# Writing TensorE's order in the first stage of a decoder layer by hand

## The chip, the cores and the metric

The kernel runs on one core of a Trainium2 chip. The time is device microseconds of one execution. A core has several engines that run side by side, each with its own queue of instructions, executed in order: TensorE (PE in the profile) multiplies matrices, VectorE (DVE) does elementwise work and reductions, ScalarE (ACT) applies functions and copies, GpSimd (POOL) does some elementwise work here, and SyncE (SP) issues most of the transfers between memory and the on-chip buffers. An instruction that needs another engine's result waits at the head of its queue, and everything behind it waits too.

## The reference

One decoder layer with three sub-layers, each followed by a residual add and a layer normalisation. `x` has the shape (8, 512, 512) and the context (8, 512, 1024).

```
q, k, v = split(x @ W_in.T + b_in)              # 16 heads of 32
p  = pos @ W_pos.T + b_pos                      # relative positions
ac = einsum('tbhd,sbhd->bhts', q + r_w_bias, k) # t, s: 8 rows of the first axis
bd = rel_shift(einsum('tbhd,rhd->bhtr', q + r_r_bias, p))
attn = softmax((ac + bd) / sqrt(32))
x1 = layernorm(x + einsum('bhts,sbhd->tbhd', attn, v) @ W_out.T + b_out)

k, v = split((ctx @ W_src.T + b_src) * mask)    # 8 heads of 64, 512 keys
q    = (x1 @ W_tgt.T + b_tgt) * mask
u    = softmax(q k / 8, masked keys left out) v
x2   = layernorm(x1 + concat(x1, u) @ W_xout.T + b_xout)

out  = layernorm(x2 + ffn(x2))                  # 512 -> 2048 -> 512, quantised to fp8 between
```

The first attention goes over the first axis, which has only 8 entries: for each of the 512 rows of the second axis, 16 heads, 8 queries and 8 keys. The second attention goes over 512 keys, with a context of 1024 features.

## The kernel before, in words

The kernel has two stages. The first does the first attention, with its output projection, residual and normalisation, and beside it the keys and values of seven of the eight contexts. The second does the rest. Only the first stage is touched.

**The attention of the first stage** goes in NJ = 4 blocks `j` of 128 rows, each with T = 8 tiles `t` of 128 x 512. For a block, TensorE computes eight key products (`ps_k`, function `project`, L212), eight query products (`ps_q`) and eight value products (`ps_v`), each of four float32 matmuls of 128x512, and for each tile a small product `bd` (L378) with the relative positions. ScalarE copies keys and values to on-chip memory. VectorE does all of the attention by elementwise work, since 8 x 8 scores for each row are too small for TensorE: for each tile it adds a bias to the query (`qw`, L374), then for each half of the heads multiplies it with all keys (`pq`, L388) and sums over 32 features (`sc`, L397); every four tiles it adds `bd` (L405). GpSimd adds a constant `gc` (L416). Then comes the softmax of the block: maximum and subtraction on VectorE (L419 on), Exp on ScalarE (L423), sum, reciprocal and division on VectorE (L425 on). Then for each tile and half the scores are multiplied with all values (`pv`, L437) and summed in three adds (L447, L450, L453), which gives `ao`.

**The output** of a tile follows: TensorE transposes `ao` in four parts (`aot`, L458), ScalarE copies the result (`aoT`, L460), TensorE multiplies it with the output weights (`po`, L463). SyncE loads the row of `x` (L472), GpSimd adds the bias `bo` to it (L473), VectorE adds `po` (L479) and takes the statistics (L98, L99). Every four tiles ScalarE and VectorE make the inverse deviations (L103, L105), VectorE normalises (L109) and ScalarE's queue stores the result to `x1d` in memory.

**The set-up** projects the positions (`pp`, L283), combines them with the query weights (`pg` L320, `pc` L330 and L332) into `gp` and `gc`, and folds the value bias through the output weights into `bo` (`pbo`, added at L357). Columns that are needed as matrices are replicated by VectorE into two tiles, `brep` and `brew` (L328, L331, L347), which are used again and again.

**The context products of the first stage.** Contexts 0 to 5 are taken in three pairs. Keys (part 0) and values (part 1) of a pair are computed in two halves with seven products each instead of eight (a Winograd scheme, L553: `py`, `pz`, `px`): 2 x 3 x 2 x 7 = 84 products, each of the size of a key product (8 records in the profile, as each float32 matmul of this form is told as two). The scheme needs sums of weights (`sums_of_a`, L134 on) and of contexts (`sums_of_b`, L140 on), made by VectorE; those of the contexts are written to memory (`td`) and read again for part 1. ScalarE moves the results out of the accumulators (`put`), VectorE adds them (`add`, L595), and ScalarE's queue stores them to `kd` and `vd`. Context 6 is done in plain form by `project_context` in eight pieces of two products' length (`psk` L158, `psv` L172); its weights take the place of the keys and values of the last block (`w6k`, `w6v`), and its context the place of the tiles of `x`. Context 7 is done in the second stage.

**What sets the order.** In the first stage the program is written tile by tile, and the context products behind all blocks; a scheduler of the programming framework then puts every engine's instructions in an order that it plans by its own estimate of their durations, with a few pieces marked `high_priority`. In the second stage the orders of TensorE, VectorE, ScalarE and SyncE are those in which the program issues the instructions (`manual_schedule`).

**Buffers.** Accumulators in the first stage: two for the products of `x` (`ps_mm`), one each for `bd`, `aot` and `po`, three for set-up and context products (`ps_kv`). `qw`, `ao` and `aoT` have two buffers each, `pq`/`pv` one, `r` four, and the tiles of `x` eight. Keys, values and scores have one buffer each, so that a block's keys can be written only when the scores of the block before are done, and its values when the last `pv` is done.

At the end of the stage, SyncE's queue waits for the last `pv` of block 3 before it loads the value weights of context 6, then come `w_src`, the second stage's weights and, by way of memory, the transposed `x1` (`x1Ts`), with which the first product of the second stage (`psq`, L824) begins.

Of the kernel before, what the change touches and what calls it, by code (L numbers as in the profile page):

```python
# [17 lines left out]
P = 128  # L18
# [24 lines left out]
def decoder_layer(  # L43
# [22 lines left out]
    nc = tc.nc  # L66

# [11 lines left out]
    def col(i):  # L79
        return colv[:, i : i + 1]  # L80
# [49 lines left out]

    A11, A12, A22, S3, S1, S2, S4 = range(7)
# [17 lines left out]
    def project_context(t, w_k, w_v, ct_of, ps_pool, ps_tag, st_pool, st_tag):  # L149
# [5 lines left out]
        def keys(o):  # L155
            ps = ps_pool.tile([P, S], F32, tag=ps_tag, name=f"psk{t}_{o}")
            for f in range(FC):
                nc.tensor.matmul(  # L158
                    ps,
                    lhsT=w_k[:, f, o * P : (o + 1) * P],  # L160
# [8 lines left out]
        def values(s):  # L169
            ps = ps_pool.tile([P, E], F32, tag=ps_tag, name=f"psv{t}_{s}")  # L170
            for f in range(FC):
# [3 lines left out]
                    rhs=w_v[:, f, :],  # L175
# [11 lines left out]
    with ExitStack() as ph:  # L187
# [33 lines left out]
        def keys_of(j):  # L221

            k_all = kvp.tile([P, T, E], F32, tag="k", name=f"k{j}")
            xts = []
            for t in range(T):
                xt = xtp.tile([P, EC, P], F32, tag="xt", name=f"xt{j}_{t}")

                (nc.sync if j else nc.scalar).dma_start(xt, xT[t, j])
                xts.append(xt)
                ps = project(xt, 1, f"k{j}_{t}")  # L230
                nc.scalar.copy(k_all[:, t, :], ps)
            return xts, k_all
# [7 lines left out]
        first = keys_of(0)  # L240
# [10 lines left out]
        with tc.tile_pool(name="setup", bufs=1) as sp:  # L251
# [26 lines left out]
            for z in (pz, pzb, zb):  # L278
                nc.gpsimd.memset(z, 0.0)
            for c in range(EC):  # L280
                pp = ps_kv.tile([P, 15], F32, tag="kv", name=f"pp{c}")
# [29 lines left out]

            one = sp.tile([P, P], F32, name="one")
            nc.gpsimd.memset(one, 1.0)
            brep = sp.tile([P, P], F32, name="brep")
            brew = sp.tile([P, P], F32, name="brew")

            for c in range(EC):
# [10 lines left out]
                nc.vector.tensor_scalar(brep, one, bqr[:, c : c + 1], None, ALU.mult)  # L328
                pg = ps_kv.tile([P, 4, 15], F32, tag="kv", name=f"pc{c}")
                nc.tensor.matmul(pg, lhsT=brep, rhs=pz[:, c], start=True, stop=False)  # L330
                nc.vector.tensor_scalar(brew, one, bwr[:, c : c + 1], None, ALU.mult)  # L331
                nc.tensor.matmul(pg, lhsT=brew, rhs=zb[:, c], start=False, stop=True)  # L332
                nc.scalar.copy(gc[:, 4 * c : 4 * c + 4, :], pg)

            for part in (0, 2):
                nc.sync.dma_start(
                    w_in[:, :, part * E : (part + 1) * E],
                    chunked(w_inT)[:, :, part * E : (part + 1) * E],
                )
            nc.scalar.dma_start(w_o, chunked(w_outT))  # L340

# [1005 lines left out]
```

## Time and profile before

| | |
|---|---|
| median of 3 runs | 2117.41 us (2115.08 to 2119.38) |
| the profiled execution, own time | 2119.34 us |
| its span, first to last instruction | 2117.6 us |
| first query add of VectorE | at 44.25 us |
| end of the last `ao` of the first stage | at 823.26 us |
| first product of the second stage | at 892.66 us |
| mean granted TensorE clock | 0.993 |
| PE, DVE, ACT, POOL busy in the span | 97%, 68%, 22%, 8% |

The busy time of PE counts a matmul from its start to its modelled end, and neighbouring matmuls overlap; back to back, a 128x512 record starts every 0.429 us while its own length is given as 0.6. A lone one therefore counts for more, and a busy share near 100% does not say that nothing more would fit. Windows give the busy time of every engine in a stretch of the span; the lists of waits give, for each engine, what it waited for at the head of its queue, with the total, the number of times and the longest. Waits of an engine that is not the bottleneck cost nothing. The costliest lines of VectorE in the first stage are L437 (64 of 2353 ns in the mean), L388 (64 of 2318 ns) and L397 (64 of 2280 ns).

### The profile page before, as it was taken

What the parts mean: (1) busy time and instruction counts of PE and PEld (TensorE: products, weight loads), DVE (VectorE), ACT (ScalarE), POOL (GpSimd) and SP (SyncE); (2) the same over time, 40 slices, a digit from 0 to 9 for tenths busy, and PEclk for the clock granted to TensorE, in tenths of its full rate; (3) what the DMA queues carried; (4) which work ended last, traced back from release to release, by engine and by line L of the source; (5) the groups of instructions that cost most, each with busy time, mean ns of one, the idle gap of its engine ahead of it and who ended that gap; (6) DMA issues with size and microseconds to landing.
All of it is one profiled execution on the core that took longest, in us unless ns stands there. A gap on an engine that the chain in (4) does not pass through costs nothing.

```text
span 2117.6 us, 17267 instructions
## 1 busy us (share of the span) xinstructions
PE 2058.4 (97%) x5768; PEld 881.4 (42%) x5768; DVE 1434.4 (68%) x2285; ACT 467.4 (22%) x955; POOL 173.3 (8%) x147
## 2 busy tenths in 40 slices
PE   9899999999999999998999999999999999999998
PEld 4444344444444444432434443434444434343443
DVE  3999999999999996057554754845747548356232
ACT  3011102110110111122223232332332323333211
POOL 0200010110012001010101111010010100000000
PEclk9999999999999999999999999999999999999999
DMA  6421341345015254576493654745636537427200
GB/s 215 177 71 40 142 151 30 120 188 194 25 55 203 94 187 156 183 194 159 109 224 91 118 131 96 138 111 95 135 88 110 139 91 143 104 65 156 53 20 20
DMA packets 246201, 255.27 MB, mean 121 GB/s; under 512 B 141024, under 2 KB 161504, under 8 KB 246112
## 3 DMA queue, kind: packets, MB, share of 16 engines
q1 hardware_dynamic: 228736, 223.45, 41.4%
q10 hardware_dynamic: 17376, 30.71, 4.1%
q8 instruction: 46, 0.75, 0.1%
q14 instruction: 43, 0.35, 0.1%
HBM read 130.36 MB, written 56.62 MB: 88 GB/s over the span
## 4 chain that ended last, share of the span: by engine, by line
PE 69%; DVE 22%; DMA 5%; issue 2%; SPq 1%; ACT 1%; POOL 0%; ACTq 0%; DVEq 0%; POOLq 0%
PE h L1036 21%; PE pox L981 5%; PE pox L969 5%; PE s L844 5%; PE av L944 5%; PE o L1053 4%; PE px L553 4%; PE psq L824 4%; DVE pq L388 4%; DVE sc L397 4%; DVE pv L437 4%; DVE pv L447 2%; PE psk L158 2%; PE psv L172 2%; PE ps_q L212 2%
## 5 line engine op out<-in xcount | busy, mean ns | idle before, releaser
L1036 PE MATMUL h<-x2T,w 128*128 128x512 f32 x1024 | 454.4, 599 | 4.3 <-DVE x2T L752 4.3
L859 DVE CUSTOM_DVE_ANT_0 pe<-s,mb 128x512 f32<-128x512 f32 x256 | 162.0, 681 | 208.8 <-PE s L844 208.8
L1036 PEld LDWEIGHTS h<-x2T,w 128*128 128x128 f32 x1024 | 192.1, 191 | 263.1 <-issue 255.7
L869 ACT ACTIVATE pe<-pe,nmax 128x512 f32<-128x512 f32 x256 | 182.2, 712 | 202.4 <-DVE nmax L859 200.2
L896 DVE STREAM_TRANSPOSE pb<-pe 128x512 f32<-128x512 f32 x256 | 159.5, 678 | 0.0
L1043 ACT ACTIVATE hq<-h,colv 128x512 fp8e4<-128x512 f32 x128 | 87.9, 687 | 294.5 <-PE h L1036 294.5
L437 DVE TENSOR_TENSOR pv<-v,sc 128x2048 f32<-128x2048 f32 x64 | 150.6, 2353 | 2.0
L388 DVE TENSOR_TENSOR pq<-qw,k 128x2048 f32<-128x2048 f32 x64 | 148.4, 2318 | 1.2
L397 DVE TENSOR_REDUCE sc<-pq 128x64 f32<-128x2048 f32 x64 | 145.9, 2280 | 1.3
L844 PE MATMUL s<-kT,qTx 64*128 64x512 f32 x512 | 128.0, 616 | 3.6 <-DVE nmax L859 3.4
L212 PE MATMUL ps_q<-w_in,xt 128*128 128x512 f32 x256 | 121.4, 604 | 5.0 <-DVE qw L374 5.0
L944 PE MATMUL av<-pT,vx 128*64 128x512 f32 x512 | 119.1, 608 | 6.3 <-DMA raw<-vd 6.3
L212 PE MATMUL ps_k<-w_in,xt 128*128 128x512 f32 x256 | 116.7, 606 | 5.4 <-DMA xt<-in_xT_dram 4.9
L884 DVE TENSOR_SCALAR pe<-pe,rden 128x512 f32<-128x512 f32 x256 | 115.4, 493 | 4.5
L463 PE MATMUL po<-w_o,aoT 128*128 128x512 f32 x256 | 117.4, 601 | 0.7 <-ACT aoT L460 0.7
L824 PE MATMUL psq<-x1Ts,w_tgt 128*128 128x512 f32 x256 | 113.8, 597 | 1.7 <-DVE x1Ts L752 1.7
L981 PE MATMUL pox<-w_xo,uT 128*128 128x512 f32 x256 | 115.2, 598 | 0.0
L969 PE MATMUL pox<-w_xo,x1Ts 128*128 128x512 f32 x256 | 114.4, 596 | 0.0
L1053 PE MATMUL o<-w2q,hq 128*128 128x512 fp8e4 x512 | 114.1, 379 | 0.0
L212 PE MATMUL ps_v<-w_in,xt 128*128 128x512 f32 x256 | 112.0, 594 | 0.0
L473 POOL TENSOR_TENSOR r<-r,bo 128x512 f32<-128x512 f32 x32 | 57.5, 1822 | 507.8 <-DMA r<-in_x_dram 368.7
L988 DVE TENSOR_TENSOR x<-pox,x 128x512 f32<-128x512 f32 x32 | 22.1, 692 | 105.6 <-PE pox L981 67.7
(142 smaller groups left out, 2165.4 us busy)
## 6 DMA issues: line engine op xcount, KB each, us to landing
pT<-pb SPq DMA_DIRECT2D x512, 128.0 KB, 2.4
ch<-in_ctxT_dram SPq DMA_DIRECT2D x24, 512.0 KB, 6.7
td<-tx SPq DMA_DIRECT2D x12, 768.0 KB, 5.7
tx<-td SPq DMA_DIRECT2D x12, 768.0 KB, 8.2
r<-in_x_dram SPq DMA_DIRECT2D x32, 256.0 KB, 3.8
x1d<-r ACTq DMA_DIRECT2D x32, 256.0 KB, 2.6
x1Ts<-x1d SPq DMA_DIRECT2D x32, 256.0 KB, 5.7
kT<-kd SPq DMA_DIRECT2D x32, 256.0 KB, 3.2
```

Of the source, the lines that this page charges most:

```text
L212: nc.tensor.matmul(ps, lhsT=xt[:, e, :], rhs=w_in[:, e, part * E : (part + 1) * E], start=(e == 0), stop=(e == EC - 1),)
L388: nc.vector.tensor_tensor(pr, qw[:, fs] .rearrange("p (h d) -> p h d", d=D1) .unsqueeze(2) .to_broadcast([P, HH, T, D1]), k_all[:, :, fs]. ...
L397: nc.vector.tensor_reduce(sc[:, t, g * HH * T : (g + 1) * HH * T], pr.rearrange("p h s d -> p (h s) d"), AX.X, ALU.add,)
L437: nc.vector.tensor_tensor(pr, v_all[:, :, fs].rearrange("p s (h d) -> p s h d", d=D1), sc[:, t, g * HH * T : (g + 1) * HH * T] .rearrange( ...
L824: nc.tensor.matmul(ps, lhsT=w_tgt[:, e, o * P : (o + 1) * P], rhs=x1T[t][:, e, :], start=(e == 0), stop=(e == EC - 1),)
L844: nc.tensor.matmul(ps[:, h, :], lhsT=qT[t][half[h], c, j * P : (j + 1) * P], rhs=kT[t, c][half[h], :], start=True, stop=True,)
L869: nc.scalar.activation(pe, pe, AF.Exp, bias=nmax[:, h : h + 1], scale=-1.0, accum_out=den[:, h : h + 1],)
L944: nc.tensor.matmul(av[half[h], :], lhsT=v[t, c][:, s, half[h]], rhs=pT[t, c][:, :, :, s, h].rearrange("p g i q -> p (g i) q"), start=(s == 0),
L969: nc.tensor.matmul(po, lhsT=x1T[t][:, e, j * P : (j + 1) * P], rhs=w_xo[:, e, :], start=(e == 0), stop=False,)
L981: nc.tensor.matmul(po, lhsT=uT[t][:, e, j * P : (j + 1) * P], rhs=w_xo[:, EC + e, :], start=False, stop=(e == EC - 1),)
L1036: nc.tensor.matmul(ps, lhsT=w1[0][:, e, n * P : (n + 1) * P], rhs=x2T[t][:, e, :], start=(e == 0), stop=(e == EC - 1),)
L1053: nc.tensor.matmul(po, lhsT=hq[t][:, c, j * P : (j + 1) * P], rhs=w2q[:, c, :], start=(c == 0), stop=(c == HC - 1),)
```

## The change

TensorE's order in the first stage is now the order in which the program issues it; VectorE, ScalarE, GpSimd and SyncE are still ordered by the scheduler. The block's work is cut into functions of one tile: `keys`, `queries_of`, `offsets`, `values`, `softmax`, `weigh`, `turn_out` (transposes and copy) and `put_out` (projection, residual, normalisation). Their bodies are those of before.

The program keeps a planned time, `clock`. A slot has one of three lengths: SCORES for a query tile, SOFTMAX for the softmax of a block, VALUES for a tile of the weighted values. In a slot the listed steps are issued, with products of `spare` set between them (the values of this block, or the keys of the next), and the rest of its length is filled from `filling`, a generator that issues one context product at a time. The generator can also say that another product has to come between (`"between"`), or that no context product may be issued for a while (a negative number).

```
        SCORES, SOFTMAX, VALUES, FULL = 11.2, 13.0, 12.4, 3.54

        def slot(length, items, left):
            begin, due = due, due + length
            steps = list(items)
            for i in range(max(len(spare) - left, 0)):
                steps.insert(2 * i + 1, None)
            for i, step in enumerate(steps):
                if step:
                    must(*step)
                elif len(spare) > left:
                    must(FULL, *spare.pop(0))
                until = begin + length * (i + 1) / len(steps)
                if step and step[1] is turn_out:
                    until = max(until, clock + 0.5)
                fill(until)
            fill(due)
```

The blocks are then written so:

```diff
+        filling.append(context_work())
+        for j in range(NJ):
+            for t in range(T) if j else range(2, T):
+                if j and t == 0:
+                    spare += [(values, j, u) for u in range(T)]
+                items = []
+                if t < T - 1:
+                    items.append((FULL, queries_of, j, t + 1))
...
+                items += [(0.9, offsets, j, u) for u in late]
+                if j and t < 2:
+                    items.insert(0, (0.9, turn_out, j - 1, T - 2 + t))
+                    items.append((FULL, put_out, j - 1, T - 2 + t))
+                slot(SCORES, items, T - 1 - t)
+            softmax(j)
...
+                spare += [(keys, j + 1, u) for u in range(T)]
+            fill(clock + FULL)
+            slot(SOFTMAX, [], max(len(spare) - 2, 0))
+            for t in range(T):
+                weigh(j, t)
+                items = []
+                if t > 1:
+                    items.append((0.9, turn_out, j, t - 2))
+                if t == T - 1:
...
+                        items.append((FULL, queries_of, j + 1, 0))
+                if t > 1:
+                    items.append((FULL, put_out, j, t - 2))
+                slot(VALUES, items, max(T - 3 - t, 0))
```

So the query of a tile is issued one tile ahead; the transposes of a tile come two slots after its weighted values, those of the last two tiles of a block in the first two query slots of the next block; and the output projection of a tile stands at the end of the slot in which the tile was transposed, behind another product.

In block 3 there are no keys of a next block. The weights for the keys of context 6 are loaded after that block's softmax and for its values at its last tile, and the four key pieces of context 6 join the filling work behind the context products. After the last slot come the turn of tiles 6 and 7, each followed by filling work and its projection, then what is left, then the four value pieces.

The set-up is cut up too: all replicated columns are made at the start in tiles of their own, and TensorE's order is keys 0 to 5, `pp` 0, key 6, `pp` 1, key 7, `pp` 2 and 3, query 0; then, in the first two query slots, combination 0, query 1, combination 1, and combination 2, query 2, combination 3, the bias product `pbo`, with value products between them. Context products may be issued from 33.0 us of planned time after that.

```diff
+            reps = []
             for c in range(EC):
+                reps.append([])
+                for n, src in (
+                    ("r", bqr[:, c : c + 1]),
+                    ("w", bwr[:, c : c + 1]),
+                    ("v", colv[:, C_BV + c : C_BV + c + 1]),
+                ):
+                    rep = sp.tile([P, P], F32, name=f"rep_{n}{c}")
+                    nc.vector.tensor_scalar(rep, one, src, None, ALU.mult)
+                    reps[c].append(rep)
...
-                nc.vector.tensor_scalar(brep, one, bqr[:, c : c + 1], None, ALU.mult)
...
+            must(1.0, project_offsets, 0)
+            must(FULL, keys, 0, T - 2)
+            must(1.0, project_offsets, 1)
+            must(FULL, keys, 0, T - 1)
+            for c in (2, 3):
+                must(1.0, project_offsets, c)
+            must(FULL, queries_of, 0, 0)
```

The context products keep their order among themselves; the generator marks the places where it yields:

```diff
+                        y = bank("py")
+                        product(y, A12, b21, True)
+                        yield FULL
+                        if i == 0 and m + part > 0:
+
+                            yield -6.0 if part else -13.0
...
+                        add(0, 0, x)
+                        store(0, 0)
+                        yield "between"
+                        product(x, S2, t2, False)
+                        yield FULL
```

The number of instructions of each kind on each engine stays as it was.

## The prediction

> **What bounds the kernel now.** I read the busy shares first, then the slices, the windows by stage, the two wait lists of the first stage, and the timeline where it ends. Shares and slices (40 slices of 52.9 us):
>
> ```profile
> PE 2058.4 (97%) x5768; PEld 881.4 (42%) x5768; DVE 1434.4 (68%) x2285; ACT 467.4 (22%) x955; POOL 173.3 (8%) x147
> ...
> PE   9899999999999999998999999999999999999998
> ...
> DVE  3999999999999996057554754845747548356232
> ```
>
> PE looks full throughout, but VectorE is full in slices 2 to 16: that is the first stage, which alone is changed. Windows (length, PE busy, PEld, DVE, ACT, POOL, clock, DMA share, GB/s) from the first query add to the last attention output, and on to the second stage:
>
> ```profile
> 44.25:823.50 779.25, 750.55 (x2031) 342.90 (x2030) 746.36 (x669) 98.62 (x171) 78.89 (x64) 1.00 0.34 117
> 823.50:892.70 69.20, 69.20 (x164) 30.50 (x163) 7.73 (x14) 6.86 (x11) 3.87 (x2) 1.00 0.63 202
> ```
>
> DVE is idle for 32.9 of 779.25 us: up to `ao` the stage goes by VectorE. Then PE alone has 69.2 us left. What each waits for (us, times, longest), PE first:
>
> ```profile
> PE aot L458 <- DVE ao L453: 10.9, 10, 2.0
> PE ps_q L212 <- DVE qw L374: 5.0, 4, 1.5
> PE ps_k L212 <- DMA xt<-in_xT_dram: 4.9, 1, 4.9
> ```
>
> ```profile
> DVE den L425 <- ACT sc L423: 8.0, 4, 2.5
> DVE mx L419 <- POOL sc L416: 7.1, 4, 1.8
> DVE qw L374 <- PE ps_q L212: 5.9, 2, 3.9
> DVE r L479 <- POOL r L473: 2.5, 3, 1.4
> DVE st L595 <- PE px L553: 1.7, 2, 1.3
> DVE w L134 <- DMA w<-in_w_srcT_dram: 1.4, 1, 1.4
> ```
>
> 15.1 us are the softmax's own chain, some 13 us are waits on other work, the rest small gaps (4.8). The end of the stage on PE's timeline:
>
> ```profile
> 838.58 26.77 PE L158 MATMUL psk<-ct,w6k 128*128 128x512 f32 x62
> 865.19 27.63 PE L172 MATMUL psv<-w6v,ct 128*128 128x512 f32 x64
> 892.66 13.90 PE L824 MATMUL psq<-x1Ts,w_tgt 128*128 128x512 f32 x32
> ```
>
> From 838.58 to 865.19 are 62 matmuls, 0.429 us each: a product of 8 matmul records is 3.43 us, a piece of context 6 (16) is 6.87.
>
> **The change, part by part.** Nothing is added to the arithmetic; the order on PE, and through it the waits, are what changes. The second stage starts at 892.66 before; I work out where it starts after.
>
> *PE alone.* 229 products x 3.43 (786) + 32 offset groups x 0.89 (28.4) + 32 groups of transposes x 0.46 (14.7) + set-up 8.8 = 838 us. PE starts at 4.93 and the first products are 2.95 slower than warm ones, so it could not be done before 846: before, PE loses 46.6 us.
>
> *DVE alone.* It keeps its instructions: 746.4 busy, less some 2.0 (replicated columns, now made before the first query: 8 of 0.28, less their overlap) and 1.4 (one `r` add with its statistics, 0.68+0.68, put off until after `ao`) = 743.0. The first query is done after 8 key products, four `pp` of 0.88 and one product: 4.93+2.95+27.4+3.5+3.4, about 42.3; qw at 42.9 (before 44.25). Softmax waits 12.7: 15.1 less 2.4, as context adds can now stand in them (bounds 10 to 15). Small gaps 4.8. So the last `ao` lands at 42.9+743.0+12.7+4.8 = 803.4 plus X, where X is what DVE waits for PE and loads (13.1 before).
>
> *Where PE is last held by DVE.* I lay the after kernel's two instruction lists side by side with these durations. Without waits, PE comes to the turn of tile 2 in block 3 only 1.8 us after `ao` (tile 3: 2.2; tiles 5 to 7: 12 to 15). DVE's softmax waits and X come on top, so PE waits there, and behind it PE has more left than DVE. `ao` of tile 2 lies five value tiles ahead of the last; one is two halves of pv, add, add, add at 4.77 plus r and statistics, by the list 54 in all: 803.4-54 = 749.4+X. Behind that turn PE has 6 groups of transposes 2.8 + 6 output products 20.6 + 13 context products 44.6 + 8 pieces 55.0 = 123.0 us. End: 872.5+X.
>
> *X, by its waits.* Third qw, behind two combines and a product on PE: 0.9. `bo` waiting for pbo, now behind the fourth combine: 2.1. Sums waiting for w and the first context loads: 1.5 (the row shows 1.4; 0 to 3). The add of block 0's first pair waiting for pz, as PE does a product in between: 3.5 by the list (nearest row 1.3; 0 to 4). Third query of block 2, behind a turn, a projection and values: 2.0. `r` behind POOL: 1.5 (row: 2.5 in three). Sum 11.5. Not counted, as PE is then 5 to 17 us ahead in the list, and so the range's upper part: in block 0 PE holds at v3 until qw of tile 3, which stands behind the first pair's sums on DVE (4 to 7.5); at px behind a DVE add (2.5); at the fourth and fifth output projection, whose single bank waits for the r adds (2.7+1.1). Everything in PE's fixed queue then stands behind them: values, context products, queries.
>
> *The tensor clock.* A 4.35 us wait before the feed-forward product costs more than itself:
>
> ```profile
> 1923.70 13.18 PE L1036 MATMUL h<-x2T,w 128*128 128x512 f32 x24 [4.35 <-DVE x2T L752]
> ```
>
> 24 at 0.43 would take 10.5; so 2.7 more, and the windows say why (granted clock is the number after POOL):
>
> ```profile
> 1920.00:1925.00 5.00, 1.30 (x2) 0.79 (x3) 2.79 (x6) 0.16 (x1) 0.00 (x0) 0.72 1.29 202
> 1925.00:1930.00 5.00, 5.00 (x8) 1.94 (x8) 4.21 (x12) 2.10 (x3) 0.00 (x0) 0.60 1.04 237
> 1930.00:1935.00 5.00, 5.00 (x14) 2.13 (x12) 1.15 (x4) 3.48 (x8) 0.00 (x0) 1.00 0.88 278
> ```
>
> In the first stage no wait of PE passes 2.2 us once it runs. The new order has two long ones by the list, both in block 3: some 16+ us at tile 0's turn (absorbed, as PE is held again) and about 6 at tile 2's, after which PE is the bound. I take 2.2 there (between 0 and 2.7). [...]
>
> *What I cost at nothing.* POOL's 32 adds (57.5 us) and their interplay with DVE: pv takes 2353 ns in the mean, 2290 undisturbed; 64 of each make 4 us, so -4 to +4. SP's queue: key tiles, `r`, sums and context loads are issued in the new order, key products follow context products, so the x tiles (bound: one 4.9 us wait, the row for xt) come up to one product earlier than needed; 0 to 3. ACT's copies, 98.6 busy of 779: 0. The loads of context 6 go ahead of `ao`'s last tiles on SP, as they do before; its keys are wanted only some 20 us behind the loads: 0 to 3. At the stage's end SP waits for the last pv before the value weights, w_src and w_tgt; x1Ts is turned by DVE at 888.8, 3.8 us ahead of 892.66. The same order remains: after the last `ao` PE has po and 8 pieces, 58.9, where before it had 69.2. If the 10 us less cover is more than the loads bear: 0 to 5. I take 0, since the other half of that chain (last `ao`, stores, loads) also comes sooner.
>
> *Sum.* 872.5+11.5+2.2 = 886.2 against 892.66: -6.5 us. The profiled execution took 2119.34 (span 2117.6 and 1.74 around it), 1.9 above the median 2117.41; I put the difference on the median: 2110.9, say 2111.
>
> **Rivals.**
> A. *DVE walks freely.* The three slot lengths leave PE ahead everywhere, X is 0 to 5 and the clock keeps up. For it: before, PE's waits on ao and qw (15.9) are symptoms of an order which is now loosened by two slots; in blocks 1 and 2 the list gives PE 15 to 30 us of slack. Against: set-up and block 0. End 872.5 to 877.5: 2097 to 2102.
> B. *No difference.* One early stall of PE (v3, 7.5) is passed on through qw: 893.7, +1.0, 2118; or the transition's loads take 5: 2116.
> C. *Slower: a convoy in block 0.* PE's order cannot step past v3, px and the two output projections, DVE then waits for the queries behind them, and passes everything on, as it is the bound until block 3. Price 7.5+2.5+3.8 = 13.8 on top: end 900.0, +7.3, 2125. It is slower than before once X plus the clock passes 20.2, by over 0.2% past 24.4. For it: in block 0 the list has only 5 us to spare at tiles 4 and 5. Against: later blocks have 15 us and more, though slack of PE's side cannot win time back for DVE.
> D. *The order does nothing.* If DVE is the bound throughout and X stays at 13.1, only the tail changes: 872.5+13.1+2.2, -4.9, 2112.5; it falls in with the forecast.
>
> **How the numbers follow.** Forecast with D (2103 to 2113) 0.42; A 0.14; B (within 0.2%, 4.2 us, about what a measurement of this kernel can tell) 0.21; C 0.23. Faster: 0.42+0.14 = 0.56. The range leaves 0.1 at each end: down to A's 2098; up, C's 2125 with 2.7 for a second cold stretch and POOL's half: 2128. The forecast's own range is 2103 to 2116.
>
> **What would show it.** Right: psq of the second stage starts at about 886; last `ao` near 815; PE's list has lost aot but for block 3, with one wait of over 10 us there and a granted clock under 1 behind it near 760; DVE's waits on PE add to about 10. Wrong: waits of qw on ps_q repeated in every block (C); PE waiting in front of psk, or psq waiting on x1Ts or w_tgt (transition); a larger mean of pv or pq (POOL); second stage not 1225 us long.

## The result, and the profile after

The changed kernel is slower: a median of 2130.4 us (2124.54 to 2131.57, six runs) against 2118.37 us in the six runs beside it, a ratio of fast runs of 1.0047 with a 95% interval of 1.0032 to 1.0061 (the two medians alone give 1.0057). Forecast were 2111 us, and at most 2128. The profiled execution took 2124.54 us, the fastest of the six. A later one of the same kernel (run e8_again) took 2129.8, and is used beside it where the difference matters.

The page of the changed kernel, busy shares and slices (40 of 53.1 us; PEclk is the granted TensorE clock in tenths):

```profile
PE 2050.7 (97%) x5768; PEld 889.9 (42%) x5768; DVE 1439.9 (68%) x2285; ACT 467.1 (22%) x955; POOL 171.5 (8%) x147
...
PE   9999999999999879998999999999999999999998
...
DVE  4999999999899997157554754835747648356232
...
PEclk9999999999999989999999999999999999999999
```

The shares say nothing: 97% and 68%, as before. The slices do: PE has an 8 and a 7 in slices 14 and 15, where it had nines, and the clock an 8. That is 690 to 796 us, block 3's softmax and its first value tiles.

Windows from the first query add to the last `ao`, and on to the second stage (length, PE busy, PEld, DVE, ACT, POOL, clock, DMA share, GB/s):

```profile
41.46:831.97 790.51, 748.59 (x2027) 353.24 (x2026) 748.46 (x657) 98.38 (x171) 77.58 (x64) 0.98 0.33 116
831.97:901.05 69.08, 68.73 (x167) 30.64 (x165) 9.71 (x17) 6.87 (x11) 3.53 (x2) 1.00 0.64 204
```

VectorE starts 2.8 us earlier than before and its last `ao` lands 8.7 us later (831.97 against 823.26); what PE has left then is as long as before, 69.1 us against 69.4. What PE waits for in the first 900 us (us, times, longest):

```profile
PE aot L337 <- DVE ao L329: 19.4, 3, 11.9
PE po L346 <- ACT aoT L339: 8.2, 9, 2.5
PE ps_k L216 <- DMA xt<-in_xT_dram: 5.1, 1, 5.1
PE ps_v L216 <- DVE qw L245: 5.0, 1, 5.0
PE po L346 <- DVE r L362: 3.8, 3, 1.6
PE px L660 <- DVE st L702: 3.4, 3, 2.4
```

and VectorE between its first query add and its last `ao`:

```profile
DVE ao L329 <- PE aot L337: 7.1, 3, 4.2
DVE den L301 <- ACT sc L299: 6.8, 4, 2.5
DVE qw L245 <- PE ps_q L216: 6.7, 5, 3.9
DVE mx L295 <- POOL sc L292: 6.5, 4, 1.8
DVE r L362 <- PE po L346: 3.3, 4, 1.5
DVE bo L560 <- PE pbo L553: 1.9, 1, 1.9
```

Before, PE waited for `ao` twelve times in this stretch, 12.5 us in all and 2.0 at the longest. Now it waits three times, 11.9 the longest, and all three stand in block 3. The timeline of PE there:

```profile
725.83 3.60 PE L660 MATMUL pz<-ch,w 128*128 128x512 f32 x8
729.26 3.60 PE L660 MATMUL px<-cl,w 128*128 128x512 f32 x8
744.78 0.69 PE L337 MATMUL aot<-ident,ao 128*128 128x128 f32 x2 [11.93 <-DVE ao L329]
749.55 0.69 PE L337 MATMUL aot<-ident,ao 128*128 128x128 f32 x2 [4.08 <-DVE ao L329]
750.92 6.10 PE L346 MATMUL po<-w_o,aoT 128*128 128x512 f32 x8 [0.68 <-ACT aoT L339]
```

After `px` at 729.26 the order has nothing until the first turn of block 3, although context products are left: that `px` is followed by the mark for a product in between, and in block 3 no values or keys remain that could stand there. The planned time moves only when something is issued, so the pauses of the generator do not run out either. And the end of the stage:

```profile
852.98 20.76 PE L162 MATMUL psk<-ct,w 128*128 128x512 f32 x48
873.58 27.63 PE L176 MATMUL psv<-w,ct 128*128 128x512 f32 x64
901.05 13.90 PE L1002 MATMUL psq<-x1Ts,w_tgt 128*128 128x512 f32 x32
```

The second stage starts at 901.05 instead of 892.66, 8.4 us later. In the repeated execution it starts at 903.55, and the stage behind it is as long as before (1224.4 against 1224.9 us), so the 10 us lie in the first stage.

**A ledger of PE.** For every matmul of the first stage I take the time from its start to the next one's start, less the median for its form; the sum is what PE loses to waits and to a lower clock. The medians add up to 837.5 us in every kernel, as the matmuls are the same, and PE begins at 4.8 to 5.1. Together with the losses that gives the start of the second stage by construction, so the agreement is no proof; the ledger only says where the time is lost. In us:

| kernel | 0-100 | 100-700 | 700-800 | later | second stage at |
|---|---|---|---|---|---|
| before | 13.4 | 30.8 | 3.7 | 2.4 | 892.7 |
| changed, first profile | 9.4 | 18.0 | 28.2 | 2.8 | 901.0 |
| changed, repeated (e8_again) | 11.9 | 18.2 | 28.2 | 2.8 | 903.5 |
| PE's order planned (e9_planned) | 4.2 | 19.0 | 8.3 | 4.1 | 878.2 |
| by hand up to block 3's softmax (e12) | 9.6 | 17.8 | 8.3 | 3.7 | 881.8 |
| by hand from there on (e13) | 3.9 | 19.0 | 29.5 | 1.8 | 896.5 |
| before, with the new set-up (e14) | 3.3 | 35.3 | 2.4 | 3.8 | 887.2 |

The change does remove losses: 12.8 us of them between 100 and 700 us, and 1.5 to 4.0 in the first 100. It loses 24.5 us more than before in the one stretch behind.

### The profile page after: what moved, and what is told of

Its sections match the earlier page's. It is cut to its first block, busy times and chain, and to the rows that moved or that the text cites. A ratio compares the mean times of both kernels' runs of the same rounds, so it can differ in the third digit from the quotient of the medians.

```text
span 2122.8 us, 17257 instructions
## 1 busy us (share of the span) xinstructions
PE 2050.7 (97%) x5768; PEld 889.9 (42%) x5768; DVE 1439.9 (68%) x2285; ACT 467.1 (22%) x955; POOL 171.5 (8%) x147
## 4 chain that ended last, share of the span: by engine, by line
PE 77%; DVE 17%; DMA 2%; issue 2%; ACT 1%; SPq 1%; POOL 0%; ACTq 0%; DVEq 0%
PE h L1214 21%; PE pox L1159 5%; PE s L1022 5%; PE pox L1147 5%; PE av L1122 5%; PE px L660 5%; PE psq L1002 5%; PE o L1231 4%; PE po L346 3%; DVE pq L249 3%; PE ps_q L216 3%; PE ps_k L216 3%; DVE pv L313 3%; PE ps_v L216 3%; DVE sc L258 3%; PE psk L162 2%
## 5 line engine op out<-in xcount | busy, mean ns | idle before, releaser
L346 PE MATMUL po<-w_o,aoT 128*128 128x512 f32 x256 | 121.5, 619 | 11.9 <-ACT aoT L339 8.2
L216 PE MATMUL ps_v<-w_in,xt 128*128 128x512 f32 x256 | 117.5, 603 | 5.0 <-DVE qw L245 5.0
L216 PE MATMUL ps_q<-w_in,xt 128*128 128x512 f32 x256 | 115.3, 593 | 1.3 <-DVE qw L245 1.3
```

The source lines that it names most:

```text
L216: nc.tensor.matmul(ps, lhsT=xt[:, e, :], rhs=w_in[:, e, part * E : (part + 1) * E], start=(e == 0), stop=(e == EC - 1),)
L346: nc.tensor.matmul(po, lhsT=aoT[t][:, c * P : (c + 1) * P], rhs=w_o[:, c, :], start=(c == 0), stop=(c == EC - 1),)
```

## The experiments

VectorE's, ScalarE's, GpSimd's and SyncE's orders are planned anew for each kernel, so a small edit moves instructions on them too; that is a limit of all the small edits below. Times are medians of four to ten runs beside runs of the kernel before; the ratio is to that kernel.

**Three buffers for `ao`**

```diff
-            ao[t] = qp.tile([P, E], F32, tag="ao", name=f"ao{j}_{t}")
+            ao[t] = qp.tile([P, E], F32, tag="ao", bufs=3, name=f"ao{j}_{t}")
```

> ao has three buffers instead of two, nothing else is changed. Theory 1 (VectorE's waits for a free ao buffer, 7.1 us in three, are passed on to the end, as VectorE holds PE at the turn of tile 2 in block 3): the waits of ao on aot vanish, the last ao lands at 824 to 826 instead of 831.96, the second stage starts at 894 to 896 instead of 901.05, time 5 to 7 us below the changed kernel. Theory 2 (VectorE only waits elsewhere, since PE is behind at those places: on ps_q, po or r): the waits move to other lines, last ao within 2 us of 832, time within 2 us of the changed kernel.

2131.05 us, 1.0059 (1.0044 to 1.0074): no gain. The waits on `aot` are gone, and the first lines of VectorE's list of waits are now

```profile
DVE qw L245 <- PE ps_q L216: 15.0, 7, 4.1
DVE den L301 <- ACT sc L299: 6.8, 4, 2.5
DVE mx L295 <- POOL sc L292: 6.5, 4, 1.8
DVE r L362 <- POOL r L356: 4.2, 3, 1.9
```

`qw` has gone from 6.7 to 15.0. The last `ao` lands at 836.15, no earlier than in the repeated execution of the changed kernel (834.47). The buffer was only the place where VectorE met PE's delay; theory 2 holds.

**Nothing held back where nothing can stand in between**

```diff
-                if clock < rest or between or not filling:
+                if ((clock < rest or between) and spare) or not filling:
```

> The pauses of the context products hold only while there are other products to put in between; so block 3's softmax and its first value slots are filled with context products. Theory 1 (the end is set by PE's tail behind the turn of tile 2 in block 3, 128.7 us, with 19.4 us of idle PE ahead of it): PE's waits on ao fall from 19.4 to under 6 us, PE's work behind that turn to about 82 us, and the stage's end is then what follows the last ao: value pieces of context 6, psq between 870 and 890, time 11 to 30 us below the changed kernel, also below the kernel before by up to 18. Theory 2 (transfers at the end of the stage set it: value weights, w_src, x1Ts behind the last pv): the idle time moves behind the last ao, PE waits for w or x1Ts there, psq stays within 4 us of 901.

2123.56 us, 1.0024 (1.0014 to 1.0035): 6.8 us below the changed kernel, less than either theory's good case. PE's waits on `ao` are gone, but the products that moved up are those behind the boundary of two pairs of contexts, whose loads have only begun:

```profile
746.91 1.02 PE L660 MATMUL py<-ch,w 128*128 128x512 f32 x2
748.55 1.13 PE L660 MATMUL py<-ch,w 128*128 128x512 f32 x2 [0.62 <-DMA ch<-in_ctxT_dram]
756.19 2.08 PE L660 MATMUL py<-ch,w 128*128 128x512 f32 x2 [6.51 <-DMA ch<-in_ctxT_dram]
761.12 2.07 PE L660 MATMUL py<-ch,w 128*128 128x512 f32 x2 [2.85 <-DMA ch<-in_ctxT_dram]
```

The four parts of `ch` land one after another, and a product issued as a whole stands before each. PE still loses 18.0 us between 700 and 800, and the first turn comes at 793.73 instead of 744.78, so VectorE waits 11.1 us for the `ao` buffer. The edit lifts the pauses wherever `spare` is empty, not in block 3 alone: between 100 and 700 us PE now waits 16.0 us in seven for VectorE's adds `st` (3.1 in two before the edit), and its losses there are 24.3 instead of 18.0. Theory 1's cause is there, its remedy is not that simple.

**Both edits**

> Both edits: three ao buffers and no pause without other products. If the two are independent, the second stage starts 5 to 7 us ahead of where it starts with the filling alone. If the ao buffers do not matter or the transfers set the end, as with the filling alone within 2 us.

2130.47 us, 1.0056 (1.0041 to 1.0071), second stage at 902.3, and so later than with the filling alone (899.3). Neither expectation was met; VectorE's waits on `ps_q` are 17.7 us here, and one wait of an `r` add on GpSimd is 10.8.

**Output turned one slot behind**

```diff
-                if t > 1:
-                    items.append((0.9, turn_out, j, t - 2))
+                if t > 0:
+                    items.append((0.9, turn_out, j, t - 1))
```

(with `put_out` and the leftover tile moved alike)

> The output is turned one slot behind the weighted values instead of two, with two ao buffers as in the changed kernel. If it is the two slots that make VectorE wait for ao buffers: the 7.1 us of ao on aot vanish, last ao at 824 to 826, time 5 to 7 us below the changed kernel, unless PE then waits for ao again, as it did before the change (10.9 us in ten), which would show as waits of aot on ao in all blocks and an end within 3 us of the changed kernel's.

2151.96 us, 1.0159 (1.0142 to 1.0176). The waits for `ao` buffers are gone, but the time is 21.6 us worse, which no case expected: PE waits 28.6 us in four for the `r` add that frees the single bank of `po`, up to 12.5 us. This part of the change, the two slots, is not what costs.

**Shorter slots**

```diff
-        SCORES, SOFTMAX, VALUES, FULL = 11.2, 13.0, 12.4, 3.54
+        SCORES, SOFTMAX, VALUES, FULL = 10.9, 13.0, 12.1, 3.54
```

> The slots are planned shorter (scores 10.9 for 11.2, values 12.1 for 12.4), so that about 9 us less of context products stand ahead of block 3's softmax. Theory A (PE holds more work per tile than VectorE's pace in blocks 0 to 2, so VectorE waits for PE there, and PE then has nothing to do in block 3's softmax): VectorE's waits on PE fall by 5 to 10 us, the last ao lands at 822 to 828 instead of 832, PE's idle time in block 3 stays at 16 to 20 or grows, and what was taken out stands behind it: second stage starts within 4 us of 901. Theory B (the slots' lengths are right, VectorE is late for other reasons): last ao within 2 us of 832, and the start of the second stage 6 to 9 us later.

2134.8 us, 1.0076 (1.0057 to 1.0096). The last `ao` lands at 831.7, the second stage starts at 910.1: theory B's outcome. Taking work out of blocks 0 to 2 does not make VectorE faster, and PE has it to do behind.

**Sums of the contexts not urgent on VectorE**

```diff
-                    with tc.high_priority():
-                        sums_of_b(
+                    sums_of_b(
```

> The sums of the contexts on VectorE are no longer marked as urgent, so that the queries' adds go ahead of them. Theory A (the end is set by block 3's starved PE): the wait of ps_v on qw in block 0 (5.0 us and 2.4 of clock behind it) goes, and the end moves by less than 3 us, as PE waits 19 us in block 3 anyway. Theory B (a convoy that begins in block 0 is passed on 1:1 through VectorE): second stage 5 to 8 us earlier. If pz then waits for sums that come late, the gain is lost to waits of pz on tx.

2124.49 us, 1.0022 (1.0012 to 1.0032), second stage at 900.8. The wait of `ps_v` on `qw` in block 0 goes (5.0), `pz` waits 6.3 for `tx` instead. The last `ao` lands 2.8 us earlier than in the repeated execution, and the median lies 5.3 us below e8_again's; beside the first profile neither the last `ao` (831.7 and 831.97) nor the second stage (900.8 and 901.05) moves. The medians suggest that the stall in block 0 is worth a part of its 7.4 us; the traces do not show how much.

**Block 3 filled with the key pieces of context 6 in between**

```diff
-                filling.append(keys_in_turn())
+                between, rest = False, 0.0
+                for _ in range(2):
+                    fill(clock + FULL)
+                    between, rest = False, 0.0
+                due = clock
...
+                spare += [(key_piece, piece) for piece in pieces[:EC]]
```

(and block 3 has no slot for its softmax any more)

> Block 3 only: the pauses are lifted for two products at its softmax, and the key pieces of context 6 serve as the products in between (they stood behind all context products). Theory A (starved PE in block 3 costs the 24 us which the new order loses between 700 and 800 us): PE's losses there fall below 12 us, the second stage starts at 880 to 892, time 8 to 20 us below the changed kernel, at or below the kernel before. Theory B (the end of the stage waits for VectorE's last ao or for the loads behind it): the losses move behind 832, start of the second stage within 5 us of 901.

2133.38 us, 1.0066 (1.0051 to 1.0081). PE's losses between 700 and 800 fall to 15.4, but 20.2 us come behind 800: the last context product ends at 869.4 rather than 838.8, the loads that need its buffer (`w_src`, and in SyncE's queue behind it `x1Ts`) start later, and `psq` waits 9.9 us, to 906.95. Theory B's place, by a mechanism of its own: here context products must be done early, since their weights' buffer is the next one's.

**The changed kernel once more**

> The changed kernel itself, unaltered, once more beside the others: its profile before had 2124.5 us, while most of its runs had 2130 to 2131. Theory A (the difference lies in the first stage, where an order that is wound up tightly on PE and VectorE passes small delays on): a profile of a 2130 us run starts its second stage at 904 to 907. Theory B (it lies in the second stage): start at 901, second stage 5 us longer than 1221.8.

2129.8 us, 1.0050 (1.0035 to 1.0065), second stage at 903.55: both theories by half. 2.5 us more are lost in the first 100 us (`ps_v` waits 6.3 us for `qw` instead of 5.0), and the second stage is 2.7 us longer than in the first profile.

**PE's order left to the scheduler**

```diff
-        ph.enter_context(tc.manual_schedule(engines={ET.PE}))
```

> The changed program with its new functions, its new set-up and its new order of writing, but TensorE's order is planned again by the scheduler as before the change (the order by hand is left out). Theory A (the hand-written order of PE is what costs): PE's losses in block 3 between 700 and 800 us fall from 28 to under 10, the second stage starts at 886 to 894, time within 4 us of the kernel before or below it, as the set-up alone brings 2.8 us. Theory B (the rearranged set-up and program cost, not the order by hand): second stage at 900 to 905, time 8 to 12 us above the kernel before.

2102.94 us, 0.9922 (0.9907 to 0.9937): theory A, and 8 us further than it had it. This one line makes the changed program 27 us faster, and 16 us faster than the kernel before. It is the best of all kernels here. Its windows for the same two stretches:

```profile
42.49:826.93 784.44, 763.02 (x2072) 358.48 (x2070) 748.94 (x661) 99.94 (x174) 75.05 (x64) 0.99 0.34 120
826.93:878.16 51.23, 51.23 (x123) 22.79 (x122) 6.15 (x12) 5.40 (x9) 3.44 (x2) 1.00 0.71 228
```

VectorE's last `ao` is 5.0 us earlier than in the changed kernel, but what PE has left then is 17.9 us shorter. PE's timeline at block 3's softmax shows what it does in that time:

```profile
730.40 3.70 PE L659 MATMUL px<-tx,w 128*128 128x512 f32 x8 [1.82 <-DVE st L701]
733.93 1.02 PE L659 MATMUL py<-ch,w 128*128 128x512 f32 x2
735.53 1.12 PE L659 MATMUL py<-ch,w 128*128 128x512 f32 x2 [0.57 <-DMA ch<-in_ctxT_dram]
737.99 1.10 PE L659 MATMUL pz<-tx,w 128*128 128x512 f32 x2 [1.33 <-DMA tx<-td]
738.92 1.88 PE L659 MATMUL px<-cl,w 128*128 128x512 f32 x4
740.64 0.38 PE L337 MATMUL aot<-ident,ao 128*128 128x128 f32 x2
```

Here the same boundary of two pairs is crossed with pieces of one matmul (two records): a quarter of `py`, of `pz`, of `px`, as the parts of `ch`, `tx` and `cl` land, and half of a turn as soon as the half of `ao` is there. Between 700 and 780 us PE waits 2.7 us for loads in four, where the whole products of e2_fill wait 10.0 in three. The loads of `ch` are issued over a like stretch in both (722.60 to 737.54 us here, 735.58 to 750.32 in e2_fill). But no run orders PE by hand in such pieces, so how much of the gain comes from the pieces, and how much from having anything there at all, is not shown.

**A block 3 in the middle of a pair**

```diff
-        SCORES, SOFTMAX, VALUES, FULL = 11.2, 13.0, 12.4, 3.54
+        SCORES, SOFTMAX, VALUES, FULL = 10.9, 13.0, 12.1, 3.54
...
-                if clock < rest or between or not filling:
+                if clock < rest or (between and spare) or not filling:
...
-            slot(SOFTMAX, [], max(len(spare) - 2, 0))
+            slot(5.0 if last else SOFTMAX, [], max(len(spare) - 2, 0))
```

(and the sums not urgent, as above)

> Three edits to the changed kernel: slots of 10.9 and 12.1 (5.0 for the last softmax), so that block 3's softmax falls in the middle of a pair of contexts, whose products need no new loads; the pause for a product in between is dropped where none is left to put in between; the sums of the contexts on VectorE are not urgent. Theory A (PE starves in block 3's softmax because what stands there is held back): PE's losses between 700 and 800 us fall from 28 to under 14, second stage at 886 to 895, time 7 to 15 us below the changed kernel. Theory B (PE's total is not the bound; the last ao or loads behind it are): second stage not under 899.

2132.9 us, 1.0067 (1.0052 to 1.0082), second stage at 908.2. Theory A's remedy fails: PE no longer waits for `ao`, but 19.1 us in ten for VectorE's adds `st` within the chain of a pair, and still 7.8 for one load. It loses 20.3 us between 700 and 800, and 40.9 instead of 18 between 100 and 700.

**Projection directly behind the turn**

```diff
                     items.append((0.9, turn_out, j, t - 2))
+                    items.append((FULL, put_out, j, t - 2))
...
-                if t > 1:
-                    items.append((FULL, put_out, j, t - 2))
```

(with the first two query slots of a block, and the filling that stood behind a turn, changed alike)

> The output projection stands directly behind the turn of its tile, with nothing in between. If the product in between hides ScalarE's copy: PE's waits of po on aoT grow from 8.2 us in nine to about 0.7 x 32 = 22, that is 14 more on PE; the end is 2 to 14 us later, by how much of it falls behind the turn of tile 2 of block 3, where PE already waits 0.7 six times (then only 2 to 4). If VectorE holds PE everywhere: within 2 us.

2165.37 us, 1.0209 (1.0188 to 1.0229). PE waits 22.3 us for `aoT` in 26, as worked out, but the end is 35 us later, not 2 to 14: VectorE's waits on `aot` (15.3) and on `ps_q` (12.1) double with it, and PE's waits for the `r` add grow from 3.8 us to 13.7. The product in between is worth having where the order is fixed.

**The hand order up to block 3's softmax, and from there on**

The first edit ends the order by hand at the softmax of block 3 (e12), the second begins it there (e13):

```diff
-        ph.enter_context(tc.manual_schedule(engines={ET.PE}))
+        by_hand = ph.enter_context(ExitStack())
+        by_hand.enter_context(tc.manual_schedule(engines={ET.PE}))
...
+            if last:
+                by_hand.close()
```

```diff
-        ph.enter_context(tc.manual_schedule(engines={ET.PE}))
...
+            if last:
+                ph.enter_context(tc.manual_schedule(engines={ET.PE}))
```

> TensorE's order is the hand-written one up to the softmax of block 3, and from there on the scheduler's. Theory A (what costs is that block 3's PE order holds its products back and then cannot split them around the turns): the 28 us lost between 700 and 800 us fall under 12, the rest stays; second stage at 884 to 890, time 2110 to 2117, most of the way from 2130 to the 2103 of the planned order. Theory B (the order of blocks 0 to 2 has already delayed VectorE): the second stage starts at 896 or later, time over 2121.

> The counterpart: the scheduler's order up to the softmax of block 3, from there on the hand-written one. Theory A: 20 us of loss in block 3 come back, second stage at 894 to 900, time 2118 to 2126. Theory B: time within 6 us of the 2103 of the planned order. If both halves cost alike, this one and its counterpart lie 8 to 18 us above 2103 each.

| PE's order | planned in block 3's end | by hand in block 3's end |
|---|---|---|
| planned in blocks 0 to 2 | 2102.94, 0.9922 | 2122.44, 1.0017 (1.0008 to 1.0026) |
| by hand in blocks 0 to 2 | 2107.59, 0.9952 (0.9933 to 0.9971) | 2129.8, 1.0050 |

The end of block 3 costs 19.5 us behind the planned blocks and 22.2 behind those by hand; the blocks ahead of it cost 4.7 and 7.4, which PE loses in the first 100 us (9.6 against 4.2 in the ledger, and 11.9 against 3.9). Theory A holds for some three quarters to four fifths of the 27 us; e12 came out 2 us better than it had it. In the windows of 700 to 800 us PE is busy (second number) for 98.90 us in the kernel before and 77.83 in the changed one:

```profile
700.00:800.00 100.00, 98.90 (x244) 42.66 (x242) 94.02 (x90) 15.43 (x24) 5.65 (x7) 1.00 0.46 160
```

```profile
700.00:800.00 100.00, 77.83 (x205) 36.22 (x204) 91.81 (x81) 10.86 (x16) 1.67 (x4) 0.88 0.33 121
```

For 95.15 in e12 (only blocks 0 to 2 by hand), and 77.13 in e13 (only the end by hand):

```profile
700.00:800.00 100.00, 95.15 (x255) 43.14 (x255) 94.93 (x87) 13.21 (x20) 1.67 (x4) 0.98 0.36 132
```

```profile
700.00:800.00 100.00, 77.13 (x204) 36.00 (x204) 91.60 (x84) 11.44 (x17) 1.66 (x4) 0.88 0.36 128
```

VectorE does nearly as much in all four (91.6 to 94.9). It is PE's time that is lost there, and it is wanted at the end: the last `ao` lands at 826.93 in e9 and at 827.40 in e13, and the second stage starts at 878.2 and 896.5.

**The set-up alone, in the kernel before**

```diff
+                    rep = sp.tile([P, P], F32, name=f"rep_{n}{c}")
+                    nc.vector.tensor_scalar(rep, one, src, None, ALU.mult)
...
-                nc.vector.tensor_scalar(brep, one, bqr[:, c : c + 1], None, ALU.mult)
-                nc.tensor.matmul(pg, lhsT=brep, rhs=pz[:, c], start=True, stop=False)
+                nc.tensor.matmul(pg, lhsT=reps[c][0], rhs=pz[:, c], start=True, stop=False)
```

(the columns of `pc`'s second product and of `pbo` alike, and the loads of the weights issued ahead)

> The kernel before with the new set-up's parts alone: all replicated columns made ahead in tiles of their own, the weights' loads issued ahead; the order is the scheduler's, and blocks and context products are written as before. If the set-up is what makes the planned form of the changed program 16 us faster than before: 8 to 16 us below the kernel before, PE's losses in the first 100 us (13.4 before) under 7. If it is the order of writing (turn two slots behind, queries ahead, context products among the slots): within 4 us of the kernel before.

2114.51 us, 0.9982 (0.9971 to 0.9994): between the two cases. PE's losses in the first 100 us fall from 13.4 to 3.3 as expected for the set-up, but 4.5 come back between 100 and 700 (35.3 against 30.8), and 4.3 us remain on the median. If the parts simply add up, some 4 of the 16 us that the change gains apart from the hand order are the set-up's, and some 12 come with the rest: queries a tile ahead, the turn two slots behind, context products written among the slots. How the 12 divide among these was not tried.

## Why the prediction was wrong

**The direction, and what the sum rested on.** The step that failed is that of tile 2 in block 3: the last `ao` at 803.4 plus X of 11.5, so at 814.9, the turn five tiles ahead at 760.9, and 123.0 us of PE behind it with 2.2 of clock. Measured: last `ao` at 831.97, that of tile 2 at 772.27, and 128.8 us from there to the second stage. So the second stage comes 14.9 us later than the 886.2 of the sum: 11.4 of them are VectorE's arrival at tile 2, and 3.6 are PE's work behind it, where each of four output projections waited 0.7 us for `aoT`, which the forecast had at nothing. The structure was right: PE is held there by VectorE, and is the bound behind it. That the sum's tail behind the last `ao` (872.5+2.2-803.4 = 71.3) comes near the 69.1 measured is partly luck, as both things that it is the difference of were too short: PE's work behind tile 2, and VectorE's five tiles (54 forecast, 59.7 measured). (The 58.9 in the paragraph on loads is not that tail: key pieces and a context product were still to come.) What was off by 17 us is VectorE's last `ao`, and X is the largest of its terms:

| term | forecast | measured |
|---|---|---|
| first qw | 42.9 | 41.5 |
| VectorE busy | 743.0 | 748.5 |
| softmax waits | 12.7 | 13.3 |
| small gaps | 4.8 | 9.4 |
| X | 11.5 | 19.3 |

*Busy*: nothing was saved on the 746.4 of before. The few instructions that left were made up by others that ran beside GpSimd: the three last context sums took 771 ns in the mean instead of 682 (twelve each, 3.2 us; the first of the four sums went the other way, 685 after 796), the normalisations 574 instead of 540, the last add to `ao` 475 instead of 445. The bound of 4 us either way, from the pv row, was too low by little. *Small gaps*: a slip of bookkeeping; 3.9 us of the 13.1 that I called waits of before belong to the first qw, ahead of the window, so the gaps were 8.4 and not 4.8. *X*: the named waits came at 0.3 (third qw; 0.9 forecast), 1.9 (`bo`; 2.1), 1.0 (query of block 2; 2.0), 1.2 (`r` on GpSimd; 1.5); those for the sums' loads (1.5) and for `pz` (3.5) did not come. Not named were 7.1 us for `ao`, though two buffers and a turn two slots behind are both in the code, 4.4 us for queries at block 3's start, and 3.3 us for `po`. e1_ao3 shows that the first of these is only where the delay shows.

**The deeper miss** is a sentence, not a term: "some 16+ us at tile 0's turn (absorbed, as PE is held again)". I saw the wait, priced it in the sum through the turn of tile 2, and never asked what the scheduler's order did at the same place. The wait had the size that I saw (11.93 and 4.08 us at the two halves of that turn), but it was not absorbed. The scheduler's order puts products there, a matmul at a time. e12 and e13 measure what the two orders differ by: 19.5 to 22.2 us. With the wait filled, a last `ao` at 826.93 is enough for 878.2 (e9_planned), and one at 830.62 for 881.8 (e12), although I had wanted it at 815 for 886.

**The rivals.** C had nearly the time (2125), and its stalls came: `ps_v` on `qw` 5.0 and the clock behind it 2.4 (5.99 instead of 3.60 us, granted clock 0.50 from 80 to 85 us), `px` 2.4, both at the size named, `po` on `r` 1.3 and 0.9, half of it. Its price was too high: the hand order in blocks 0 to 2, with all of these, costs 5 to 7 us (e12 against e9, and e8_again against e13), lost in block 0 as C had it, and not 13.8. So its time was near by luck: the larger loss is in block 3, where C had none. A was not seen: X was 19.3. B's first case (one stall passed on) is part of what blocks 0 to 2 cost. Loads at the end of the stage, B's second case, did not delay it: `psq` follows `psv` without a wait. D had the order do nothing; it costs 27 us (e9_planned against e8_again).

**The clock.** The waits came as forecast, one over 10 us at tile 0's turn and one at tile 2's (3.35, where about 6 was forecast). I took 2.2 us behind the latter and nothing behind the former. Windows of the changed kernel (granted clock is the number after POOL):

```profile
743.00:748.00 5.00, 0.69 (x2) 0.29 (x2) 4.86 (x5) 0.00 (x0) 0.00 (x0) 0.50 0.47 182
748.00:752.00 4.00, 1.77 (x4) 0.86 (x5) 3.86 (x5) 0.59 (x1) 0.00 (x0) 0.50 0.00 0
752.00:757.00 5.00, 5.00 (x9) 2.14 (x8) 4.50 (x4) 0.00 (x0) 0.00 (x0) 0.62 0.00 0
757.00:762.00 5.00, 5.00 (x13) 2.14 (x12) 4.91 (x7) 0.59 (x1) 0.00 (x0) 1.00 0.59 202
```

The clock is at half, and comes back some 5 us after the projection's start at 750.92: it is 0.50 from 754 to 755 us, 0.60 in the next and 1.00 from 756 on. The product at 750.92 took 6.10 instead of 3.70 us, that at 773.43 took 5.09: 2.4 and 1.4 us. The 2.2 was my choice between 0 and the 2.7 of the feed-forward product; no run shows it, and behind tile 2, where it stood in the sum, the 1.4 was measured.

The clock fell at a shorter wait too, of 2.53 us in block 2, where the projection stood directly behind its turn, on the same timeline:

```profile
619.64 5.19 PE L346 MATMUL po<-w_o,aoT 128*128 128x512 f32 x8 [2.53 <-ACT aoT L339]
```

1.5 us more than 3.70, with a granted clock of 0.71 from 618 to 621 us. And the kernel before had a dip in the first stage too, behind a wait of 2.24 us for `tx` that ended at 78.58:

```profile
78.00:80.00 2.00, 1.42 (x2) 0.64 (x3) 2.00 (x2) 0.00 (x0) 0.00 (x0) 0.74 1.05 388
80.00:82.00 2.00, 2.00 (x4) 0.87 (x3) 2.00 (x4) 0.00 (x0) 0.00 (x0) 0.50 0.89 328
```

The prediction overlooked it, and had no term for the clock behind short waits.

**What held.** PE's waits on `ao` are gone but for block 3; the wait over 10 us and the dip of the clock stand where they were put (the dip at 745 and 773; 760 was named). The transition costs nothing. Two of the signs that were named failed: the last `ao` came at 832 instead of near 815, and VectorE's waits on PE came to 19 us instead of about 10.

## What to carry to other kernels

Before an order is written by hand, read what the planner's order does in the places where the bound engine will wait, and in what pieces: here the whole products of e2_fill waited 10.0 us for loads that land in quarters, the planner's pieces in e9_planned 2.7, and in the changed kernel PE stood idle for 4.08 us between the halves of a turn. What the order by hand did in one stretch of 100 us outweighed all that the rest of the change gained elsewhere. Look at the last round of a loop by itself: what fills the waits of the other rounds (the next block's keys) is missing there, and a rule like "not without something in between" then stops everything. And when a change has several parts, take the one line away that switches its main part off: that run showed that the rest of this change is worth 16 us.

## What the runs showed of the hardware

Beside GpSimd's adds `r`, which read two tiles of the on-chip buffer, in these runs VectorE's adds of two such tiles took 2.1 times as long in the median, and its multiplications of 128x2048 1.46 times; its adds with one input in an accumulator, and its sums, took no longer (counts below). VectorE in the changed kernel:

```profile
92.34 2.28 DVE L249 TENSOR_TENSOR pq<-qw,k 128x2048 f32<-128x2048 f32 x1
94.55 1.75 DVE L145 TENSOR_TENSOR tx<-ch,tx 128x512 f32<-128x512 f32 x1
96.22 1.75 DVE L146 TENSOR_TENSOR cl<-ch,cl 128x512 f32<-128x512 f32 x1
97.90 1.75 DVE L147 TENSOR_TENSOR tx<-ch,tx 128x512 f32<-128x512 f32 x1
99.57 2.27 DVE L258 TENSOR_REDUCE sc<-pq 128x64 f32<-128x2048 f32 x1
```

and GpSimd:

```profile
92.56 8.21 POOL L356 TENSOR_TENSOR r<-r,bo 128x512 f32<-128x512 f32 x4 [90.42 <-DVE tx L144]
```

The three adds take 1.75 us instead of 0.68; the multiplication `pq`, which began 0.22 us ahead of GpSimd, and the sum `sc` are not slowed (2.28 and 2.27 us, with medians of 2.29 for both). I counted the instructions of the first stage that lie at least 95% within GpSimd's adds `r`, in the sixteen profiles together, and call slow what took over 1.1 times the median of its form. Slow were 116 of 126 adds of two tiles of the buffer (2.1 times in the median) and 70 of 78 multiplications of 128x2048 (1.46 times); of 150 adds with one input in an accumulator and of 150 sums and statistics, none. GpSimd's times are rough, and why the remaining few stayed fast is open. No run tried the first attention's small scores on TensorE.
